# Four instructions in other places of the engines' lists: exponentials, a layer norm's shift, bias pieces and LSTM weight sums

## The chip, the cores and the metric

The kernel runs on one core of a Trainium2 chip. The metric is the time of one execution on the device in microseconds, as the median of several runs. All data are fp32. A core has five engines with a queue of instructions each: TensorE (matmul; in the profile PE, and PEld for its loads of weights), VectorE (DVE), ScalarE (ACT), GpSimd (POOL) and SyncE (SP, which issues the DMA transfers here).

## What is computed

A stack of four graph layers on x of 128 graphs with 64 nodes and 256 features, with one 64x64 adjacency. Each layer is "x = x + layer(relu(layernorm(x)))".

```python
# --- layer 0 ---   two graph convolutions, then LSTMs over windows of 1, 2, 3, 4 nodes
h = relu(einsum('ts,bsh->bth', adj, h @ Wg0 + bg0))
h = relu(einsum('ts,bsh->bth', adj, h @ Wg1 + bg1))
for p in range(1, 5):            # the last hidden state replaces the window's last node
    h = h.at[:, idx, :].set(lstm_last(Wih[p-1], Whh[p-1], ..., windows(h, p)))
# --- layer 1 ---   normalized adjacency, two linear layers with batch norm
# --- layer 2 ---   three weights, for diagonal, upper and lower part of adj, and a bias
out = adj_0 @ (x @ W[0]) + adj_1 @ (x @ W[1]) + adj_2 @ (x @ W[2]) + bias
# --- layer 3 ---   masked attention over the 64 nodes of a graph
scores = q @ k.T * scale + adj_mask          # causal
y = softmax(scores) @ v @ Wo
```

## The kernel before

The 8192 rows are cut into 16 tiles of 512 rows (number s). There are three long stages: graph rounds (layer 0 up to the LSTM, one tile each round), the LSTM steps with layer 1 after them, and a last stage for layers 2 and 3, which takes the tiles in 8 pairs.

The order of each engine's instructions is planned by hand. Every piece of work is entered in a list with a planned time, `at(t, function, ...)`; the list is sorted by this time and the functions are called in that order. A planned time is therefore no moment, only a place: it decides which instruction stands before which in the queue of its engine. What an instruction waits for is set by its data.

```python
def at(t, fn, *args):
    events.append((t0 + t, len(events), fn, args))
...
for _, _, fn, args in sorted(events, key=lambda e: e[:2]):
    fn(*args)
```

**A graph round** (`t0 = 10 * s`). Layer norm: statistics on VectorE, the root on GpSimd (power of -0.5), the shift on VectorE, relu on ScalarE:

```python
def root(qs):
    rn = v["rn"][:, 0, qs]
    nc.vector.tensor_scalar_add(rn, v["mv"][:, qs, 1], EPS)
    nc.gpsimd.tensor_tensor(rn, rn, mhalf[:, : qs.stop - qs.start], ALU.pow)      # L318
def shift(qs):
    nc.vector.scalar_tensor_tensor(v["rn"][:, 1, qs], v["mv"][:, qs, 0], -1.0,     # L321
                                   v["rn"][:, 0, qs], op0=ALU.mult, op1=ALU.mult)
def relu(q):
    nc.scalar.activation(v["h"][:, q, :], v["xt"][:, q, :], AF.Relu, ...)          # L325
```

Then the first convolution (`aggregate0`, L333, with a ScalarE copy out of the bank, L337; `weigh`, L343; `weighed`, the add of a bias out of the bank, L349 on VectorE; `relu1`, L354 on ScalarE), the second aggregation with the same two lines, and the second weight in a form of Strassen's with seven products, one round later:

```python
for k in range(2):
    at(late + 6.56 + 1.72 * k, weigh, k)
    at(late + 8.3 + 1.75 * k, weighed, k)
    at(late + 8.9 + 1.75 * k, relu1, k)
late += ROUND          # 10
...                    # aggregate0 of "g1" with its copies
for k in range(4):
    at(late + (7.2, 7.9, 8.0, 8.05)[k], sums, k)     # GpSimd, L364
late += ROUND
for t, name, j in ((0, "c", 2), (0.43, "a", 1), (1.75, "b", 5), (2.18, "a", 6),
                   (3.5, "b", 3), (3.93, "a", 7), (6.1, "a", 4)):
    at(late + t, product, name, j)                   # TensorE, L372
at(late + 0.5, begun, 0, 0, "c")                     # VectorE, L379
at(late + 0.9, add, 0, 0, "a")                       # VectorE, L386
at(late + 2.3, begun, 1, 1, "b")
...
if s == 9:
    for k in range(4):
        at(0.6 + 1.6 * k, lambda k=k: weight_sum(wih0[0], k))   # GpSimd, L279
```

Product a6 adds to bank a, which `add(0, 0, "a")` must have read before. b5 and the products before it don't wait for that add.

**A pair of the last stage** (`t0 = 52.5 * i`, tiles 2i and 2i+1). In the order of one tile: norm of x2 to h2 (root L967, shift L970, relu L974), the bias added to x2 by GpSimd (`biased`, L987), the graphs of layer 2 (`graphs3`, matmuls L999, copies L1004 on ScalarE and VectorE), the weights (L1011), the sum (`weighed`, L1017), norm to h3, transposes (L1024), then seven products for q k (`qproduct`, L1051) with ScalarE copies (`qcopy`, L1055) and VectorE adds (`qadd`, L1058) and four products for v (`hv`, L1075, copied at L1079), scores (L1085), mask (L1090), row maximum (L1095), exponentials, their transposes, and the last product:

```python
def exps(q):
    nc.scalar.activation(v["sc"][:, q, :], v["sc"][:, q, :], AF.Exp,              # L1098
                         bias=v["mx"][:, 0, q : q + 1], accum_out=v["mx"][:, 1, q : q + 1])
...                       # turn_e: transposes L1106, turned_e: copy L1110; attend: L1116, attended: L1121
u = 0.43
for k, (name, j) in ((0, ("c", 2)), (1, ("a", 1)), (4, ("b", 5)), (5, ("a", 6)),
                     (8, ("b", 3)), (9, ("a", 7)), (13, ("a", 4))):
    at(t_QH + k * u, qproduct, name, j)
for q, k in enumerate((2, 6, 10, 14)):
    at(t_QH + k * u, hv, q)
at(t_QH + 2 * u, qcopy, 0, 0, "a")
at(t_QH + 3 * u, qadd, 0, 0, "c")
at(t_QH + 5.1 * u, qcopy, 1, 1, "b")
at(t_QH + 6.1 * u, qcopy, 0, 1, "a")
at(t_QH + 8 * u, hv_copy, 0)
at(t_QH + 10.1 * u, qadd, 1, 1, "a")
at(t_QH + 10.2 * u, qadd, 0, 1, "b")
at(t_QH + 14.1 * u, qcopy, 1, 0, "a")
at(t_QH + 16 * u, hv_copy, 1)
at(t_S, scores)
at(t_S + 2, masked)
at(t_soft, largest)
for q in range(Q):
    at(t_soft + 0.7 + 0.6 * q, exps, q)
... # turn_e at t_E, attend and attended from t_O
```

Products b3 and a7 need that `qcopy` has read bank b and bank a. The even tile's scores and exponentials (t_S = 40.0, t_soft = 42.7) lie among the odd tile's products (t_QH = 42.0).

Of the kernel before, what the change touches and what calls it, by code (L numbers as in the profile page):

```python
# [20 lines left out]
def kernel(ctx: ExitStack, tc: tile.TileContext, a: dict, out: bass.AP):  # L21
# [255 lines left out]
    def weight_sum(w, k):  # L277
        op = nc.gpsimd.tensor_sub if k else nc.gpsimd.tensor_add
        op(*(w[:, m] for m in ((S1, A21, A22), (S2, S1, A11), (S3, A11, A21), (S4, A12, S2))[k]))  # L279
# [10 lines left out]
    ROUND, HALF = 10.0, SUP // 2  # L290
    with tc.tile_pool(name="pa", bufs=2) as pa, tc.tile_pool(name="pax", bufs=3) as pax:
        events, wih0, made = [], [], []

        def graph_part(s):
            t0, v = ROUND * s, {}

            def at(t, fn, *args):
                events.append((t0 + t, len(events), fn, args))
# [118 lines left out]
                    at((-15.1, -14.5, -13.1, -12.5)[q], stats, q)  # L417
            for qs, t in halves:
                at(t, root, qs)
                at(t + 1.4, shift, qs)  # L420
                for q in range(qs.start, qs.stop):
                    at((2.7 - ROUND if s == 1 else t + 1.5) + 0.6 * (q - qs.start), relu, q)
            late, end = 0, s == NS - 1
            for c in range(KC):
                at(late + 0.86 + 1.75 * c, aggregate0, "g0", "h", c)
# [6 lines left out]
            for c in range(KC):  # L432
                t = (0.86, 2.6)[c] if end else 4.35 + 0.89 * c
# [38 lines left out]
                at(5.0, lambda: normalize(made[0]))  # L472
            if s == 9:
                for k in range(4):
                    at(0.6 + 1.6 * k, lambda k=k: weight_sum(wih0[0], k))

        for s in range(NS):
            graph_part(s)
# [60 lines left out]
    def at(t, fn, *args):  # L539
        events.append((t, len(events), fn, args))  # L540
# [169 lines left out]
    t = 0.0  # L710
    wt[0][0].append(wih0[0])
    for p in range(1, NL + 1):
# [8 lines left out]
        for k in range(0, len(pairs), 2):  # L721
            sts = [{"blk": blk, "N": blk[0][2] * GB, "p": p, "pool": pool}
                   for blk, pool in zip(pairs[k : k + 2], (lh0, lh1))]
            for j in range(p):
                for st in sts:
# [4 lines left out]
                    t = step(t, st, j, j == p - 1, l, wt[l], turn)  # L730
# [187 lines left out]
    NP = NS // 2  # L918
    with tc.tile_pool(name="pc", bufs=2, reuse_waits="tile") as pc, \
# [3 lines left out]
        def rest(s, at, only_pair, t_T, t_n, t_G, t_W, t_h, t_QH, t_S, t_soft, t_E, t_O, end):  # L923
# [6 lines left out]
            def q2s(k):  # L930
                return slice(2 * k, 2 * k + 2)
# [20 lines left out]
            def norm(src, tag, halves, t_rows, t_relu):  # L952

                def new():
                    v["st"] = pc.tile([P, Q, 6], F32, tag="ln_st", name="ln_st", bufs=4)
                    v["mv"] = pc.tile([P, Q, 2], F32, tag="ln_mv", name="ln_mv", bufs=4)
                    v["rn"] = pc.tile([P, 2, Q], F32, tag="ln_rn", name="ln_rn", bufs=4)
                    v[tag] = pc.tile([P, Q, D], F32, tag=tag, name=tag)

                def stats(q):  # L960
                    nc.vector.bn_stats(v["st"][:, q, :], v[src][:, q, :])
                    nc.vector.bn_aggr(v["mv"][:, q, :], v["st"][:, q, :])
# [11 lines that stand above are left out]
                    nc.scalar.activation(v[tag][:, q, :], v[src][:, q, :], AF.Relu,  # L974
                                         bias=v["rn"][:, 1, q : q + 1], scale=v["rn"][:, 0, q : q + 1])

                at(t_rows[0] - 0.01, new)
                for q in range(Q):
                    at(t_rows[q // 2] + 0.6 * (q % 2), stats, q)
                for k, qs in enumerate((q2s(0), q2s(1)) if halves else (slice(0, Q),)):  # L980
                    at(t_relu[k] - 1.5, root, qs)
                    at(t_relu[k] - 0.1, shift, qs)
                    for q in range(qs.start, qs.stop):
                        at(t_relu[k] + 0.6 * (q - qs.start), relu, q)
# [150 lines left out]
            if first_:  # L1135
                norm("x2", "h2", True, (t_T + 0.455, t_T + 1.8), (t_T + 3.2, t_T + 4.6))
                for q in range(Q):
                    at(t_T + 7 + 0.7 * q, biased, q)
            else:
                norm("x2", "h2", False, (t_n, t_n + 1.2), (t_n + (11.9 if s % 2 and s > 1 else 4.1),))  # L1140
                for q in range(Q):
                    at(t_n + (14.5 if s % 2 else 10.5) + 0.7 * q, biased, q)
            for k in range(4):
                at(t_G + 0.8 * k, graphs3, *((k % 2, k // 2) if first_ else (k // 2, k % 2)))
            for k in range(2):
# [33 lines left out]
            at(t_S + 2, masked)  # L1179
            at(t_soft, largest)  # L1180
            for q in range(Q):
                at(t_soft + 0.7 + 0.6 * q, exps, q)
            for k, qs in enumerate((q2s(0), q2s(1)) if end else (slice(0, Q),)):
                at(t_E + 0.2 * k, turn_e, qs)
                at(t_E + 0.2 * k + 0.1, turned_e, qs)
# [4 lines left out]
        for i in range(NP):  # L1190
            t0, first_, end = PERIOD * i, i == 0, i == NP - 1

            def at(t, fn, *args, t0=t0):
                events.append((t0 + t, len(events), fn, args))

            rest(2 * i, at, i, -8.6 if first_ else -40.2, -38.3, 0, (7.0, 12.6), 29.0, 32.6, 40.0, 42.7,
                 46.3 if end else 46.5, 50.4 if end else 48.85, False)
            if first_:
                at(-7.6, weight_product, 2, wo, wvo)
            rest(2 * i + 1, at, i, -3.0 if first_ else -27.6, 1.5 if first_ else -25.4, 12.3 if first_ else 3.5, (17.8, 26.5), 39.1,  # L1200
                 (42.0, 45.4, 48.7, 49.6, 52.1) if end else 42.0, 46.7 if end else 50.6,
                 49.5 if end else 59.5, 53.0 if end else 64.7, 53.8 if end else 75.6, end)
        for _, _, fn, args in sorted(events, key=lambda e: e[:2]):
            fn(*args)
# [38 lines left out]
```

## Time and profile before

The median of three runs is 1910.28 us (1909.95 to 1910.47). The profiled execution spans 1908.6 us.

| what | value |
|---|---|
| ScalarE copy of half a bank (L1055) | 0.37 us each |
| exponential of 128x128 (L1098) | 0.39 us, and 0.19 us to read its sum |
| GpSimd root of 128x4 (L967) | 1.0 us |
| bias piece on GpSimd (L987), 128x256 | 0.7 us |
| LSTM weight sum on GpSimd (L279), 128x512 | 1.3 us |
| graph rounds repeat every | 10.49 us |
| pairs of the last stage repeat every | 52.49 us |

How to read the views: the page's first part gives, for each engine, its busy time, the share of the span and the number of instructions. A list of waits says which engine and line waited for which other, with the total in us, how often, and the longest. A timeline gives start (us from the start of the span), length (us), engine, line, operation, what is written and read, the shape, and in brackets the idle time before the instruction with what ended it. Busy time over a stretch is given for all engines in one row. L numbers are lines of the kernel before.

### The profile page before, as it was taken

The numbers are of one execution on the slowest core, as the hardware profiler recorded it, in microseconds if no ns is written. First come the engines' busy times: TensorE is split into PE (matmuls) and PEld (weight loads), VectorE is DVE, ScalarE is ACT, GpSimd is POOL, SyncE is SP. The second block draws the span as 40 slices with busy tenths as digits, with TensorE's granted clock in tenths as the row PEclk, the third lists the DMA queues.
The fourth block names the chain that finished last, engine by engine and source line by source line (L and its number), as shares of the span: only waits on it lengthen the run. The fifth ranks groups of instructions, "written<-read, shape, count | busy, mean of one in ns | idle before, by whom it ended". The sixth has DMA issues, their size and how long they took to land.

```text
span 1908.6 us, 19724 instructions
## 1 busy us (share of the span) xinstructions
PE 1872.3 (98%) x7112; PEld 1174.0 (62%) x7112; DVE 1142.5 (60%) x2264; ACT 890.0 (47%) x1539; POOL 612.5 (32%) x491
## 2 busy tenths in 40 slices
PE   8999999999999999999999999999999999999999
PEld 7887444444445666665444444555444888888887
DVE  6765777634546445435633334588786767666664
ACT  5765667534435444434533333444574433443442
POOL 4341322443324432422522224533053411211120
PEclk9999999999999999999999999999999999999999
DMA  4110000100001000000000001233100011111101
GB/s 138 56 56 1 1 1 15 30 1 0 1 0 45 1 0 1 1 0 23 0 0 1 1 0 35 87 111 110 64 1 22 23 45 45 45 34 45 45 23 34
DMA packets 49539, 54.34 MB, mean 28 GB/s; under 512 B 3105, under 2 KB 44833, under 8 KB 49441
## 3 DMA queue, kind: packets, MB, share of 16 engines
q1 hardware_dynamic: 48976, 52.87, 8.8%
q8 instruction: 57, 0.93, 0.2%
q14 instruction: 42, 0.34, 0.1%
q10 hardware_dynamic: 464, 0.20, 0.0%
HBM read 36.28 MB, written 16.78 MB: 28 GB/s over the span
## 4 chain that ended last, share of the span: by engine, by line
PE 88%; DVE 6%; POOL 3%; ACT 3%; issue 1%; DMA 0%; ACTq 0%; DVEq 0%; POOLq 0%
PE ps L605 34%; PE ps L611 19%; PE ps L1011 8%; PE ps L521 6%; PE ps L841 5%; PE ps L999 2%; PE ps L1075 2%; PE ps L1051 2%; PE ps L333 2%; PE ps L372 2%; PE ps L219 1%; PE ps L1116 1%; POOL t L364 1%; DVE tq L1038 1%; PE ps L1085 1%; PE ps L229 1%
## 5 line engine op out<-in xcount | busy, mean ns | idle before, releaser
L627 DVE TENSOR_TENSOR gate<-gate,ps 128x512 f32<-128x512 f32 (+2 forms) x378 | 224.1, 620 | 446.1 <-PE ps L611 366.8
L605 PE MATMUL ps<-tx,wih 128*128 128x512 f32 (+2 forms) x1008 | 446.8, 542 | 2.8 <-ACT gate L630 1.2
L605 PE MATMUL ps<-hT,wih 128*128 128x512 f32 (+2 forms) x756 | 338.5, 541 | 0.0
L630 ACT COPY gate<-ps 128x512 f32<-128x512 f32 (+2 forms) x252 | 134.5, 534 | 378.5 <-PE ps L611 325.0
L605 PEld LDWEIGHTS ps<-tx,wih 128*128 128x128 f32 x1008 | 190.5, 190 | 193.0 <-issue 130.8
L623 ACT ACTIVATE gate<-gate,lbias 128x512 f32<-128x512 f32 (+2 forms) x252 | 216.7, 860 | 157.5 <-DVE gate L627 157.5
L611 PE MATMUL ps<-h,whh 128*128 128x512 f32 (+2 forms) x576 | 256.6, 527 | 0.0
L605 PEld LDWEIGHTS ps<-hT,wih 128*128 128x128 f32 x756 | 143.6, 190 | 141.6 <-issue 79.6
L611 PE MATMUL ps<-th,whh 128*128 128x512 f32 (+2 forms) x432 | 192.5, 527 | 0.0
L1011 PE MATMUL ps<-wl,ag 128*128 128x256 f32 x768 | 172.1, 380 | 0.0
L611 PEld LDWEIGHTS ps<-h,whh 128*128 128x128 f32 x576 | 109.4, 190 | 100.2 <-issue 76.5
L650 POOL TENSOR_TENSOR gate<-gate 128x1024 f32<-128x1024 f32 (+2 forms) x36 | 71.8, 2016 | 304.7 <-ACT gate L623 304.7
L1011 PEld LDWEIGHTS ps<-wl,ag 128*128 128x128 f32 x768 | 143.4, 190 | 20.2 <-ACT ag L1004 1.8
L650 POOL TENSOR_TENSOR cell<-gate 128x1024 f32<-128x1024 f32 (+2 forms) x36 | 79.4, 2227 | 175.2 <-ACT gate L623 175.2
L967 POOL TENSOR_TENSOR ln_rn<-ln_rn,mhalf 128x4 f32<-128x4 f32 (+1 forms) x33 | 32.8, 994 | 311.0 <-DVE ln_rn L966 310.5
L611 PEld LDWEIGHTS ps<-th,whh 128*128 128x128 f32 x432 | 82.1, 190 | 75.2 <-issue 57.4
L974 ACT ACTIVATE h<-x,ln_rn 128x256 f32<-128x256 f32 x128 | 68.2, 593 | 104.2 <-DVE ln_rn L970 104.2
L521 PE MATMUL ps<-ag,w 128*128 128x512 f32 x256 | 112.3, 592 | 0.0
L650 POOL TENSOR_TENSOR cell<-gate,cell 128x1024 f32<-128x1024 f32 (+2 forms) x32 | 65.1, 2052 | 109.4 <-ACT gate L623 109.4
L630 DVE COPY gate<-ps 128x512 f32<-128x512 f32 (+2 forms) x126 | 78.6, 624 | 20.8 <-PE ps L611 20.8
L655 ACT ACTIVATE gate<-cell 128x1024 f32<-128x1024 f32 (+2 forms) x72 | 68.1, 952 | 29.5 <-POOL cell L650 29.5
L623 ACT ACTIVATE gate<-ps,lbias 128x512 f32<-128x512 f32 (+2 forms) x126 | 79.6, 632 | 3.9 <-PE ps L611 1.0
(213 smaller groups left out, 2820.4 us busy)
## 6 DMA issues: line engine op xcount, KB each, us to landing
xt<-in_x_dram SPq DMA_DIRECT2D x30, 512.0 KB, 4.4
x1d<-xt SPq DMA_DIRECT2D x16, 512.0 KB, 3.0
x<-x1d SPq DMA_DIRECT2D x16, 512.0 KB, 5.1
out_dram<-x SPq DMA_DIRECT2D x15, 512.0 KB, 3.2
wih<-in_WihT_dram SPq DMA_DIRECT2D x16, 256.0 KB, 4.8
whh<-in_WhhT_dram SPq DMA_DIRECT2D x12, 256.0 KB, 5.2
xt<-in_x_dram SPq DMA_DIRECT2D x8, 128.0 KB, 3.8
wl<-in_W_dram SPq DMA_DIRECT2D x3, 256.0 KB, 3.1
```

The lines of the kernel that those rows point to most:

```text
L333: nc.tensor.matmul(p_[:, ts(q, P)], v[h][:, q, ts(c, P)], adjT_bd, start=True, stop=True)
L521: nc.tensor.matmul(p_, con["w1"][:, c, ts(o, P)], ag[:, c, :], start=(c == 0), stop=(c == KC - 1))
L605: nc.tensor.matmul(wide(p_[:, :N]), wih[0][:, OF[k], gi, :], x_, start=first_, stop=(j == 0), skip_group_check=True)
L611: nc.tensor.matmul(p_[:, :N], whh[0][:, OF[k], gi, :], h_, start=False, stop=True, skip_group_check=True)
L623: nc.scalar.activation(to, r[bank_][:, :N] if bank_ else to, fn, bias=lbias[:, l, m : m + 1])
L627: nc.vector.tensor_add(slot(n, hc), slot(n, hc), r[bank_][:, :N])
L630: op(slot(n, hc), r[bank_][:, :N])
L650: fn(*((t["G"] if isinstance(t, dict) and "G" in t else st["c"])[:, n, :, : st["N"]] for t in tiles))
L655: nc.scalar.activation(o_, c, AF.Tanh)
L841: nc.tensor.matmul(banks[name], w2[:, OF[j], k, :], x_, start=(new and k == 0), stop=(k == 1), skip_group_check=True)
L974: nc.scalar.activation(v[tag][:, q, :], v[src][:, q, :], AF.Relu, bias=v["rn"][:, 1, q : q + 1], scale=v["rn"][:, 0, q : q + 1])
L1011: nc.tensor.matmul(v["W"][:, q, :], v["ag"][:, c, m, ts(2 * k + q, P)], wl2[m][:, c, :], start=(n == 0), stop=(n == 3 * KC - 1))
```

## The change

It moves four things in the lists and leaves the computation and the number of instructions as they were.

- In the graph rounds the shift of the layer norm and its relus are entered 1.6 later, from the third tile on, so that VectorE's and ScalarE's queues have other work before them while GpSimd forms the root.
- The LSTM weight sums on GpSimd get other slots in the tenth round.
- In the last stage the exponentials of the even tile are entered 1.4 later (not in the last pair), behind ScalarE's copies of the odd tile's banks. The transposes of the exponentials and the product after them move back by about 2, and the odd tile's scores move ahead of that product.
- The bias pieces of the odd tiles are entered 3.5 later.

```diff
             for qs, t in halves:
                 at(t, root, qs)
-                at(t + 1.4, shift, qs)
+                at(t + (1.4 if s < 2 else 3.0), shift, qs)
                 for q in range(qs.start, qs.stop):
-                    at((2.7 - ROUND if s == 1 else t + 1.5) + 0.6 * (q - qs.start), relu, q)
+                    at((2.7 - ROUND if s == 1 else t + (1.5 if s == 0 else 3.1)) + 0.6 * (q - qs.start), relu, q)
...
             if s == 9:
                 for k in range(4):
-                    at(0.6 + 1.6 * k, lambda k=k: weight_sum(wih0[0], k))
+                    at(1.4 + 1.3 * k, lambda k=k: weight_sum(wih0[0], k))
...
                 for q in range(Q):
-                    at(t_n + (14.5 if s % 2 else 10.5) + 0.7 * q, biased, q)
+                    at(t_n + (18 if s % 2 else 10.5) + 0.7 * q, biased, q)
...
             for q in range(Q):
-                at(t_soft + 0.7 + 0.6 * q, exps, q)
+                at(t_soft + (0.7 if s % 2 or only_pair == NP - 1 else 2.1) + 0.6 * q, exps, q)
...
     # even tile: ..., t_h, t_QH, t_S, t_soft, t_E, t_O
             rest(2 * i, at, i, ..., 29.0, 32.6, 40.0, 42.7,
-                 46.3 if end else 46.5, 50.4 if end else 48.85, False)
+                 46.3 if end else 48.46, 50.4 if end else 50.85, False)
     # odd tile: t_QH, t_S
-                 (42.0, 45.4, 48.7, 49.6, 52.1) if end else 42.0, 46.7 if end else 50.6,
+                 (42.0, 45.4, 48.7, 49.6, 52.1) if end else 42.0, 46.7 if end else 48.9,
```

## The prediction

> **What bounds the kernel now.** I read the page's first part and its waits first, then asked for busy time by stage, then for the chain of waits and the timeline of one repeat in each stage that the change touches.
>
> ```profile
> PE 1872.3 (98%) x7112; PEld 1174.0 (62%) x7112; DVE 1142.5 (60%) x2264; ACT 890.0 (47%) x1539; POOL 612.5 (32%) x491
> ```
>
> ```profile
> 20.00:176.00 156.00, 151.78 (x915) 135.72 (x915) 101.19 (x265) 104.07 (x171) 60.60 (x78) 1.00 0.18 52
> 176.00:1476.00 1300.00, 1292.57 (x3670) 663.75 (x3669) 737.39 (x1200) 613.25 (x933) 459.21 (x283) 1.00 0.06 20
> 1476.00:1909.00 433.00, 416.03 (x2469) 363.84 (x2467) 291.63 (x752) 162.35 (x417) 84.30 (x106) 1.00 0.12 38
> ```
>
> The first line says that TensorE is the bound; nothing can be won that is not an idle moment of PE. The three stages (columns: stretch, length, then busy time of PE, PEld, DVE, ACT, POOL) say where idle moments are: 4 us in the graph rounds (20 to 176), 7 us in the LSTM with the first products after it (176 to 1476), which no edited line touches except one weight sum ahead of it, and 17 us in the last stage. Each matmul row is drawn about 0.17 us too long (a 0.43 us pair of rows shows as 0.60), so a gap is really larger than the idle time says; I count gaps from start to start instead.
>
> What ends those gaps, from the list of waits, PE alone (us in total, times, longest):
>
> ```profile
> PE ps L1051 <- ACT qk L1055: 7.9, 7, 1.1
> PE ps L372 <- DVE h L386: 4.1, 12, 1.3
> ```
>
> The change goes at exactly these two. The first is once in each pair of the last stage but the last pair (seven times), the second once in nearly every graph round.
>
> **What the Trainium skill says.** "PSUM — Partial Sum Buffer", section "Engine vs sequencer instructions": the queues of ScalarE, VectorE and GpSimdE are strict FIFO. So an instruction that waits holds back all that follow it, though they are ready, and moving it later in the list can free them; but a move that passes no other instruction of its own engine does nothing. The trace agrees: the 0.16 us shift at 67.10 below holds a ready add behind it. "SBUF — State Buffer", "Who interferes with whom": a VectorE instruction with two SBUF inputs contends with a GpSimd instruction that reads SBUF, and the loser blocks for the whole instruction. The trace agrees: the same shift takes 0.16 us alone and 1.22 us beside a weight sum. The same two sections give me all I use; for every duration I take the trace.
>
> **The graph rounds: shift and relu later (s ≥ 2).** The timeline of one round, us from the start, us long, engine, line:
>
> ```profile
> 66.05 1.01 POOL L318 TENSOR_TENSOR ln_rn<-ln_rn,mhalf 128x4 f32<-128x4 f32 x1
> 66.36 1.03 PE L372 MATMUL ps<-g,wg 128*128 128x256 f32 x4
> 67.10 0.16 DVE L321 SCALAR_TENSOR_TENSOR ln_rn<-ln_mv,ln_rn 128x4 f32<-128x4 f32 x1 [1.07 <-POOL ln_rn L318]
> 67.18 0.68 DVE L349 TENSOR_TENSOR h<-ps,rsb 128x512 f32<-128x512 f32 x1
> 68.11 0.60 PE L372 MATMUL ps<-t,wg 128*128 128x256 f32 x2
> 68.35 0.42 DVE L386 TENSOR_TENSOR h<-h,ps 128x256 f32<-128x256 f32 x1
> 68.92 0.67 PE L372 MATMUL ps<-t,wg 128*128 128x256 f32 x2 [0.21 <-DVE h L386]
> ```
>
> GpSimd's root (L318) stands behind its four sums and ends at 67.06. DVE's shift (L321) waits for it, and behind it in DVE's queue stand `weighed(1)` (L349), `begun` (L379) and the `add` (L386) that product a6 needs. PE could have begun a6 at 68.11 + 0.43 = 68.54; it began at 68.92, and paid 0.08 more for restarting (the next row begins 0.51 and not 0.43 later): 0.46 us lost. By the plan's times modulo the round of 10, the shift moves from 9.5 to 1.1: behind `weighed(1)` (0.05), `begun` (0.5) and `add` (0.9). `weighed(1)`'s matmuls end at 66.36, 66.56 with the 0.20 that such a hand-over takes here; then 0.6 + 0.4 + 0.1 + 0.42 in DVE's queue gives 68.1, and 0.15 to PE 68.25, before 68.54. The wait is gone with 0.3 us to spare. The relus go to 1.2 to 3.0, about a microsecond later in fact; the first matmul that reads them is at 77.72, six microseconds after they end, and ScalarE has four short copies beside them.
>
> The 12 waits: at 27.00 it is 27.00 − 26.06 = 0.94 us; at 37.44, 0.32; nine of 0.46 = 4.1; and the one beside the LSTM weight sums:
>
> ```profile
> 98.52 3.84 POOL L279 TENSOR_TENSOR wih<-wih 128x512 f32<-128x512 f32 x3
> 98.59 1.22 DVE L321 SCALAR_TENSOR_TENSOR ln_rn<-ln_mv,ln_rn 128x4 f32<-128x4 f32 x1 [1.08 <-POOL ln_rn L318]
> ```
>
> Here the shift is blocked by the weight sum (1.22 us), and a6 begins at 101.47 instead of 100.02: 1.5 us with the restart. Moved behind the add it may still be blocked, but then only the next `begun`, which has 0.4 to 0.6 us of slack; I leave 0.2 us of the 1.5 there. One round more gains: in round 10, relus of s = 2 stand before `relu1(1)` (18.15), which PE waits for at 18.82; with the relus behind it, PE is next held by the g0 copy, which ends about 0.8 us earlier by ScalarE's list. Sum: 0.94 + 0.32 + 4.1 + 1.3 + 0.8 = **7.5 us**.
>
> **The weight sums at s = 9.** From 0.6 + 1.6k to 1.4 + 1.3k. On GpSimd they stand after the root at 8.1 of the round before and before the sums at 7.2, in the old and in the new slots. A planned time is only a place in the list, so GpSimd's list does not change, and the instructions are on no other engine: **0 us**.
>
> **The bias pieces.** For odd s from t_n + 14.5 to t_n + 18. From the second pair on this is 45.1 to 47.2 of a pair instead of 41.6 to 43.7, and GpSimd has nothing between 37.5 and the next pair's 16.8: same list, **0 us**. Only s = 1 differs: its pieces 1 to 3 fall behind the root of h3 (19.9) of the first pair. That root began when DVE's input came, not when GpSimd was free, so it gains nothing; `weighed` of s = 1 then waits for piece 1, at about 1508.15 instead of 1508.03. I put 0.1 us against it.
>
> **The exponentials behind the bank copies.** One pair:
>
> ```profile
> 1632.15 0.69 DVE L1095 TENSOR_REDUCE mx<-sc 128x4 f32<-128x512 f32 x1
> 1632.87 0.40 ACT L1098 ACTIVATE sc<-sc,mx 128x128 f32<-128x128 f32 x1 [2.07 <-DVE mx L1095]
> 1633.66 0.35 ACT L1055 COPY qk<-ps 128x256 f32<-128x256 f32 x1
> 1634.06 0.70 PE L1051 MATMUL ps<-h3T,aqk 128*128 128x256 f32 x2 [1.13 <-ACT qk L1055]
> 1634.31 0.35 ACT L1055 COPY qk<-ps 128x256 f32<-128x256 f32 x1
> 1634.71 0.70 PE L1051 MATMUL ps<-tq,aqk 128*128 128x256 f32 x2
> ```
>
> ScalarE sits 2.07 us before the first exponential of the even tile because the row maximum is late, and the copies of banks b and a of the odd tile, ready since about 1631.7 and 1632.1, stand behind it. PE finishes `hv(1)` at 1631.90 + 0.86 = 1632.76 and waits for the first copy to 1634.06 (1.30 us). b3 and a7 then take 1.35 us by the chain's own starts (a7 waits for the second copy, and both restart cold), where the same four rows without a wait take 0.86: 0.49 more. So 1.30 + 0.49 = 1.8 us stand in each pair.
>
> After: copies at 1631.7 and 1632.1, end 1632.45; b3 at 1632.76, a7 at 1633.19, hv at 1633.62, a4 at 1634.48. a4 needs DVE's add of bank a: 1633.62 + 0.20 + 0.41 + 0.15 = 1634.4, just in time. The exponentials still begin at 1632.87 (two take 0.79), the hv copy lies between (0.5), the last ends at about 1635.05. The transposes of the exponentials now stand behind the last hv, at 1635.78: 0.7 us to spare. The odd scores come next (48.9, ahead of attend at 50.85): their copy is done at about 1635.5, they run from 1636.2 to 1638.0, attend to 1639.7, and graphs of the next pair begin there, where they began at 1641.45. What this may give back: DVE's first graph copy (52.5) stands before `attended(1)` (52.61), so the bank of the second attend is free only at about 2.4 us after the graph stage begins, and the eighth graph bank needs it at 2.2: 0.2 us. Net 1.6 us. In the first pair the exponential's table load (1.28 us, at 1526.1, hidden in the wait now) comes behind the copies, and pushes the exponentials past the transposes by some 0.3 us: net 1.3. The last pair keeps its old times. Sum: 6 × 1.6 + 1.3 = **10.9 us**.
>
> **Total**: 7.5 + 10.9 − 0.1 = 18.3 us; 1910.3 − 18.3 = 1892.0.
>
> **Rivals.**
> (1) *The wait is only exchanged.* In the last stage the row maximum comes no earlier; if PE's next need, a4's add or the transposes, waits instead, little comes out. For it: the a4 margin is 0.1 us. Against it: the transposes stand 0.7 us after the last exponential. With half the gain lost there, 1897.
> (2) *Buffers pass it on.* The graph stage starts 1.7 us earlier and meets DVE's `attended` and its own copies; PE could stall on banks for more than the 0.2 us I allow. For it: copies run at PE's pace there (ScalarE waits 0.17 us for each). 0.5 us a pair would make 1894.
> (3) *The moved relus collide.* In the graph rounds g0's second copy now stands behind three relus of 0.5 us; if the weights that read it waited, the round would keep its 10.49 us, and the time would be about 1899. Against it: the copy would end near 71.0 and is read at 73.4.
> (4) *Bias and weight sums do matter*, through the shared port rather than the list. I see no way while GpSimd's list is unchanged.
>
> **Range and chances.** Losing one of the two large terms in part gives the upper end, 1898; all waits gone with no give-back (1.8 × 7 + 8) gives 1889 to 1890, and a little for gaps I did not count 1888. All of PE's idle time in both stages is about 30 us, so 2% (38 us) is out of reach: faster by over 2% 0.01, within 2% 0.985, slower by over 2% 0.005.
>
> **What would show it.** Graph rounds 10.03 us apart instead of 10.49 and no a6 waiting on L386; shift rows without a wait. In the last stage pairs some 50.9 us apart instead of 52.49, no L1051 waiting for L1055, the exponentials still ending the row maximum's wait. GpSimd's rows as before but for the first pair. The LSTM stage unchanged, only earlier by 7 to 8 us. Wrong would be: pairs at 52 us with PE waiting for L1098 or L1121, or rounds that stay at 10.4 us with a wait on L337.

## The result, and the profile after

The changed kernel takes 1891.24 us (median of 4 runs, 1890.40 to 1891.49) where the kernel before takes 1910.38: a ratio of 0.9899, 95% interval 0.9882 to 0.9917, about 19 us. The profiled span went from 1908.6 to 1889.8 us.

First part of the page of the changed kernel, and its busy time over the three stages (stretch, length, busy time of PE, PEld, DVE, ACT, POOL):

```profile
PE 1865.3 (99%) x7112; PEld 1174.5 (62%) x7112; DVE 1141.4 (60%) x2264; ACT 891.6 (47%) x1539; POOL 611.9 (32%) x491
...
20.00:168.50 148.50, 148.07 (x910) 136.45 (x911) 99.95 (x264) 104.42 (x172) 60.61 (x78) 1.00 0.18 54
168.50:1468.00 1299.50, 1292.07 (x3667) 663.33 (x3666) 737.35 (x1200) 613.16 (x933) 458.36 (x283) 1.00 0.06 20
1468.00:1890.00 422.00, 413.03 (x2471) 364.20 (x2469) 291.78 (x752) 163.71 (x417) 84.62 (x106) 1.00 0.12 39
```

Every engine does the same number of instructions in nearly the same busy time. The stretches are cut at about the same places of the program in both kernels. By these cuts the graph rounds lost 7.5 us and show almost no idle PE now (148.07 of 148.50), the LSTM stretch is as long as it was, and the last stage lost 11 us.

One graph round of the changed kernel, from its timeline; the rows answer to those shown of before:

```profile
53.26 1.00 POOL L318 TENSOR_TENSOR ln_rn<-ln_rn,mhalf 128x4 f32<-128x4 f32 x1
53.57 1.03 PE L372 MATMUL ps<-g,wg 128*128 128x256 f32 x4
53.77 0.69 DVE L349 TENSOR_TENSOR h<-ps,rsb 128x512 f32<-128x512 f32 x1 [0.53 <-PE ps L343]
54.95 0.42 DVE L386 TENSOR_TENSOR h<-h,ps 128x256 f32<-128x256 f32 x1
55.29 0.16 DVE L321 SCALAR_TENSOR_TENSOR ln_rn<-ln_mv,ln_rn 128x4 f32<-128x4 f32 x1
55.32 1.03 PE L372 MATMUL ps<-t,wg 128*128 128x256 f32 x4
```

`weighed(1)` (L349) now waits only for its own matmuls and begins 0.20 us after the four rows at 53.57 do (before: 0.82). The add (L386) ends at 55.37, the shift stands behind it and waits for nothing. Products b5 and a6 run as one block of four rows at 55.32, with no gap between them. From one such block to the next it is 10.05 us: the rows of L343 that open the weights lie at 50.28, 60.33, 70.37, 80.42 in the chain of waits.

One pair of the last stage of the changed kernel, from its timeline:

```profile
1620.92 0.81 ACT L1055 COPY qk<-ps 128x256 f32<-128x256 f32 x2 [0.87 <-PE ps L1051]
1621.40 0.69 DVE L1095 TENSOR_REDUCE mx<-sc 128x4 f32<-128x512 f32 x1
1622.02 0.59 PE L1051 MATMUL ps<-h3T,aqk 128*128 128x256 f32 x2
1622.12 0.40 ACT L1098 ACTIVATE sc<-sc,mx 128x128 f32<-128x128 f32 x1 [0.39 <-DVE mx L1095]
1622.45 0.59 PE L1051 MATMUL ps<-tq,aqk 128*128 128x256 f32 x2
...
1625.04 0.60 PE L1106 MATMUL ps<-ident,sc 128*128 128x128 f32 x4
```

The row maximum comes no earlier in the pair than before. But both bank copies are done before ScalarE begins to wait for it, so b3 and a7 follow each other by 0.43 us. ScalarE's own wait for the maximum shrank from 2.07 to 0.39 us because it works during it; the transposes (L1106) stand late enough that the last exponential is through. Busy time over one whole pair, first of the kernel before, then of the changed one:

```profile
1588.96:1641.45 52.49, 51.36 (x309) 45.45 (x309) 36.57 (x94) 20.00 (x52) 10.10 (x12) 1.00 0.13 41
```

```profile
1578.20:1629.08 50.88, 50.88 (x309) 45.46 (x308) 36.59 (x95) 20.24 (x52) 10.08 (x12) 1.00 0.13 42
```

The same 309 matmul rows, in 50.88 us instead of 52.49, and no idle PE drawn.

### The profile page after: what moved, and what is told of

Same layout as the page of the kernel before. It is cut to its first block, busy times and chain, and to the rows that moved or that the text cites. A ratio compares the mean times of both kernels' runs of the same rounds, so it can differ in the third digit from the quotient of the medians.

```text
span 1889.8 us, 19741 instructions
## 1 busy us (share of the span) xinstructions
PE 1865.3 (99%) x7112; PEld 1174.5 (62%) x7112; DVE 1141.4 (60%) x2264; ACT 891.6 (47%) x1539; POOL 611.9 (32%) x491
## 4 chain that ended last, share of the span: by engine, by line
PE 94%; DVE 3%; ACT 1%; POOL 1%; DMA 0%; issue 0%; ACTq 0%; DVEq 0%; POOLq 0%
PE ps L605 34%; PE ps L611 19%; PE ps L1011 8%; PE ps L521 6%; PE ps L841 5%; PE ps L1075 3%; PE ps L343 3%; PE ps L333 3%; PE ps L372 2%; PE ps L1051 2%; PE ps L999 2%; PE ps L1085 2%; PE ps L219 2%; PE ps L1116 1%; PE ps L1024 1%; PE ps L229 1%
## 5 line engine op out<-in xcount | busy, mean ns | idle before, releaser
L974 ACT ACTIVATE h<-x,ln_rn 128x256 f32<-128x256 f32 x128 | 68.3, 594 | 103.1 <-DVE ln_rn L970 103.1
L521 PEld LDWEIGHTS ps<-ag,w 128*128 128x128 f32 x256 | 47.6, 190 | 54.5 <-issue 52.1
```

What stands on the lines that cost most here:

```text
L521: nc.tensor.matmul(p_, con["w1"][:, c, ts(o, P)], ag[:, c, :], start=(c == 0), stop=(c == KC - 1))
```

## The experiments

The theory: two waits of TensorE were queue waits. An instruction that waits for slow work (GpSimd's root, the row maximum) stood in its engine's queue ahead of ready ones that TensorE needed. Moving shift and relus, and moving the exponentials with what follows them, accounts for all; the bias pieces and the weight sums change nothing. The rivals: the parts only work together; ScalarE's relus rather than VectorE's shift were the obstacle; TensorE's new order has a worth of its own; the bias pieces matter by blocking VectorE (rival 4 of the prediction).

| run | edit | median us | kernel before, measured beside it | ratio (95%) |
|---|---|---|---|---|
| e1 | shift and relus | 1902.72 | 1911.01 | 0.9956 (0.9944 to 0.9969) |
| e2 | exponentials and reorder | 1899.85 | 1911.01 | 0.9941 (0.9929 to 0.9954) |
| e3 | bias pieces, weight sums | 1911.08 | 1911.01 | 1.0001 (0.9993 to 1.0009) |
| e4 | relus alone | 1911.35 | 1911.01 | 1.0003 (0.9994 to 1.0011) |
| e5 | exponentials alone (one too late) | 1900.22 | 1910.79 | 0.9947 (0.9934 to 0.9959) |
| e6 | reorder alone | 1910.99 | 1910.79 | 1.0001 (0.9993 to 1.0009) |
| e7 | e1 and e2 together | 1891.49 | 1910.79 | 0.9900 (0.9887 to 0.9914) |
| e8 | the changed kernel, one more copy later | 1889.94 | 1910.79 | 0.9893 (0.9877 to 0.9908) |
| e9 | before, root twice | 1928.48 | 1910.64 | 1.0090 (1.0074 to 1.0107) |
| e10 | the changed kernel, root twice | 1892.23 | 1910.64 | 0.9901 (0.9886 to 0.9916) |
| e11 | exponentials alone, all in time | 1902.51 | 1910.96 | 0.9955 (0.9942 to 0.9969) |

**e1, shift and relus alone.**

```diff
-                at(t + 1.4, shift, qs)
+                at(t + (1.4 if s < 2 else 3.0), shift, qs)
-                    at((2.7 - ROUND if s == 1 else t + 1.5) + ..., relu, q)
+                    at((2.7 - ROUND if s == 1 else t + (1.5 if s == 0 else 3.1)) + ..., relu, q)
```

> The kernel before with the later shift and relus of the graph rounds alone. Queue theory (the shift that waits for GpSimd's root held three VectorE instructions and through them product a6): rounds 10.05 us apart instead of 10.49, no a6 waiting on L386, about 1902.7 us (7.6 less). Rival (the four moves only work together, or a later stage eats the gain): 1907 or more. The last stage keeps its pairs of 52.49 us.

It is 8.3 us less than the kernel before that was measured beside it. Rounds are 10.05 us apart, the list of waits has no L372 any more and still has the seven of L1051, and pairs stay at 52.5 us. The gain of this part stands alone.

**e2, exponentials and reorder alone.**

```diff
-                at(t_soft + 0.7 + 0.6 * q, exps, q)
+                at(t_soft + (0.7 if s % 2 or only_pair == NP - 1 else 2.1) + 0.6 * q, exps, q)
-   even tile: t_E 46.5, t_O 48.85     odd tile: t_S 50.6
+   even tile: t_E 48.46, t_O 50.85    odd tile: t_S 48.9
```

> The kernel before with the later exponentials and the new places of their transposes, the odd scores and the attend product alone. Queue theory: pairs 50.88 us apart, about 1.6 us less in each of seven pairs, 1899.2 us (11.1 less), graph rounds still 10.49 us. Rival (the bias pieces of GpSimd were part of it through the shared port): pairs above 51.2 us, 1902 or more.

It is 11.2 us less, with pairs 50.88 us apart and eleven of the twelve waits of L372 still there. The bias pieces were not part of it. The two parts add: 8.3 + 11.2 = 19.5 us, and both together (e7) gave 19.3.

**e3, bias pieces and weight sums alone**, and **e7, all but these.**

```diff
-                    at(0.6 + 1.6 * k, lambda k=k: weight_sum(wih0[0], k))
+                    at(1.4 + 1.3 * k, lambda k=k: weight_sum(wih0[0], k))
-                    at(t_n + (14.5 if s % 2 else 10.5) + 0.7 * q, biased, q)
+                    at(t_n + (18 if s % 2 else 10.5) + 0.7 * q, biased, q)
```

> The kernel before with the later bias pieces and the LSTM weight sums in other slots alone. Queue theory: GpSimd's list is the same but for three pieces in the first pair, so 1910.3 us within 0.4. Rival (the pieces run at other moments and block VectorE less): 1 to 3 us less, 1907.5 to 1909.5.

> The kernel before with shift and relus, exponentials and the reorder, but with the bias pieces and the weight sums in their old places. Queue theory: as the changed kernel, 1891.3 us within 0.4. Rival (bias and weight sums matter once the waits are gone): 1893 or more.

There is no difference either way: 1911.08 against 1911.01, and without these edits 1891.49 (the changed kernel took 1891.24). The order of GpSimd's rows in the traces says why. It differs from that of the kernel before in one place, the first pair, where three pieces of the second tile stand behind one more root; the weight sums stand where they stood. In the timeline of e3 the weight sums still begin as the root ends, 0.99 us after its start, as they did before (97.53 and 98.52):

```profile
98.31 1.02 POOL L318 TENSOR_TENSOR ln_rn<-ln_rn,mhalf 128x4 f32<-128x4 f32 x1
99.30 5.08 POOL L279 TENSOR_TENSOR wih<-wih 128x512 f32<-128x512 f32 x4
```

**e4, relus later, shift in its old place.** The edit is the second pair of lines of e1.

> The kernel before with only the relus of the graph rounds later, the shift in its old place. Queue theory (VectorE's queue held by the shift is the cause): nothing changes in the rounds, 10.49 us apart, 1910.3 us within 0.5. Rival (ScalarE's relus ahead of the bank copies were the cause): about 1903 to 1905 us.

Nothing came out, and L372 waits for L386 twelve times, 4.6 us in all. ScalarE's relus were not the obstacle. They read the shift's result, so they come later when it does; the shift without a new place for the relus was not run.

**e9 and e10, the root twice**, in the kernel before and in the changed one.

```diff
+                v["rx"] = pa.tile([P, Q], F32, tag="ln_rx", name="ln_rx", bufs=3)
...
                 nc.vector.tensor_scalar_add(rn, v["mv"][:, qs, 1], EPS)
+                if s > 1:
+                    nc.gpsimd.tensor_tensor(v["rx"][:, qs], rn, mhalf[:, : qs.stop - qs.start], ALU.pow)
                 nc.gpsimd.tensor_tensor(rn, rn, mhalf[:, : qs.stop - qs.start], ALU.pow)
```

> The kernel before with GpSimd's root of the graph rounds done twice (from the third tile on; the first result goes to a tile that nobody reads), so that it ends 1.0 us later. Queue theory: the shift and what stands behind it come 1.0 us later, and a6 with them, in 12 rounds: rounds 11.5 us apart, about 1922 us. Rival (GpSimd's root is not on the path): 1910 to 1912.

> The changed kernel with the root twice in the same way. Queue theory: the shift now stands behind the add, about 1.0 us after the root ends, so the whole extra microsecond is hidden: 1891.2 us within 1, rounds 10.05 us apart. Rival: the late root costs here too, 1897 or more.

This tests the mechanism itself: if the shift no longer stands ahead of the add, a slower root must be free. It nearly is (1892.23, 1.0 us more than the changed kernel's median), while the kernel before pays 17.8 us. The chain of waits of the kernel before shows how the root sets the length of a round (main pieces of one round):

```profile
66.10 0.98 POOL ln_rn L318
67.10 0.16 DVE ln_rn L321
68.35 0.43 DVE h L386
68.92 0.67 PE ps L372 x2
72.33 0.59 ACT g L337
74.49 2.10 POOL t L364 x3
76.58 0.98 POOL ln_rn L318
```

It is a closed loop through four engines: root, shift and add, product a6, the copy out of the bank, GpSimd's sums, and the next root. The loop takes 76.58 − 66.10 = 10.48 us, the length of a round, so a longer root lengthens every round by as much. In the changed kernel the chain runs through matmuls alone in nearly all of these rounds. Timeline of e9 (three edited lines shift the numbers by 3: L321 is the second root, L324 the shift, L389 the add, L375 the products):

```profile
74.92 1.01 POOL L321 TENSOR_TENSOR ln_rn<-ln_rn,mhalf 128x4 f32<-128x4 f32 x1
75.97 0.16 DVE L324 SCALAR_TENSOR_TENSOR ln_rn<-ln_mv,ln_rn 128x4 f32<-128x4 f32 x1 [2.85 <-POOL ln_rn L321]
77.22 0.42 DVE L389 TENSOR_TENSOR h<-h,ps 128x256 f32<-128x256 f32 x1
77.79 0.67 PE L375 MATMUL ps<-t,wg 128*128 128x256 f32 x2 [1.66 <-DVE h L389]
```

and of e10:

```profile
74.85 1.01 POOL L321 TENSOR_TENSOR ln_rn<-ln_rn,mhalf 128x4 f32<-128x4 f32 x1
75.45 0.42 DVE L389 TENSOR_TENSOR h<-h,ps 128x256 f32<-128x256 f32 x1
75.90 0.17 DVE L324 SCALAR_TENSOR_TENSOR ln_rn<-ln_mv,ln_rn 128x4 f32<-128x4 f32 x1
```

In e9 VectorE sits idle for 2.85 us before the shift, the add begins 1.25 us after the shift, and TensorE waits 1.66 us for it. In e10 the add runs at 75.45 while the second root is still at work; that root ends at 75.86, just as the shift comes up.

The 12 us that I expected for e9 were too few, though its rounds are as long as expected. From its chain, the roots of five rounds and one run of matmuls:

```profile
51.38 1.02 POOL ln_rn L321
62.97 1.02 POOL ln_rn L321
74.92 1.02 POOL ln_rn L321
86.51 1.02 POOL ln_rn L321
98.10 1.02 POOL ln_rn L321
...
116.89 1.72 PE ps L336 x8
```

Most rounds are 11.59 us long, 1.10 more than before, which is the second root (the first begins at 73.83, the second at 74.92: 1.09). The total is larger for three reasons. Thirteen rounds grew and not twelve: about 14.2 us. In two of them, the first and the one beside the weight sums, TensorE waited 1.86 and 2.37 us for the add, and the clock that it was granted, which the profile gives as a share of full speed, then read 0.50 (30.5 to 32.5 us, and 115.8 to 118.3), so that eight rows of L336 took 1.72 us where they take 0.89 otherwise; that cost another 1.66 us in each. In the other eleven rounds the waits were 1.09 to 1.66 us and the clock read 1.00; why it fell in those two was not tested. The third reason is the round shown above, which took 11.95 us: the second of GpSimd's sums began 0.50 us after the copy that it waits for, and 0.14 us after it in the next round. Its cause stays open. Together this is the 17.9 us by which the thirteen rounds of the profiled execution grew.

In e10 the rounds are 10.05 us apart as in the changed kernel, but for the first (10.15) and the one beside the weight sums (10.41 instead of 10.27). So the rounds account for 0.24 us of the 1.0; the profiled executions differ by 0.5 us, and the other 0.3 lies ahead of the first round, where all versions scatter.

**e6, the reorder of TensorE alone; e5 and e11, the exponentials alone.** e6 has the new t_E, t_O and t_S of e2 without its first edit; e5 has only that first edit. In e5 the fourth exponential's time (46.6) is just past its transposes' (46.5). So e5 leaves out the last exponential of the even tile in what it transposes: the last quarter is the masked scores, and TensorE doesn't wait for the fourth exponential. e11 has all four in time, by a spacing of 0.55; the order in every engine's list is that of e5.

> The kernel before with the transposes of the exponentials, the odd scores and the attend product in their new places, the exponentials in the old. My theory: products b3 and a7 wait for the bank copies as before, and nothing else waited, so 1910.3 us within 0.5. Rival (the new order of TensorE is itself worth something): 1 to 4 us less.

> The kernel before with the exponentials later, but their transposes, the odd scores and the attend product in their old places. My theory: the wait for the bank copies goes, but the transposes now stand right behind the third hv product and wait some 0.6 us for the last exponential: about 1.1 us less a pair, nothing in the first (table load), so some 7 us less, 1903.5 us. Rival 1 (the reorder is not needed): 1899. Rival 2 (without it the wait is only exchanged): 1909 or more.

> As e5_exps_alone, with all four exponentials ahead of their transposes in the list (spaced 0.55 instead of 0.6), so that the transposes wait for the fourth too; the order of every engine's instructions is that of e5. My theory: the transposes, right behind the third hv product, now wait some 0.6 us for the last exponential, in six pairs (in the first the table load makes it more): some 3.5 us above e5, 1903.7 us. Rival (the last exponential is not on TensorE's path even there, the reorder is not needed): 1900.2 us as e5.

The reorder alone is worth nothing: PE's wait for the copies is as before (7.9 us, 7 times). The exponentials alone bring 8.5 us (e11), with pairs of 51.16 us; with the reorder 11.2 (e2) and 50.88. So the reorder is needed for the remaining 2.7 us, and e5, which took away the data dependence and not the place, has pairs of 50.89. Which of its parts does it, the later transposes or the earlier odd scores, was not run separately; the wait that it removes is that of the transposes. I had expected a stall of 0.6 us a pair in e11; it is 0.28. The timeline of e11 shows why:

```profile
1632.89 0.89 PE L1106 MATMUL ps<-ident,sc 128*128 128x128 f32 x4
1632.91 0.39 ACT L1098 ACTIVATE sc<-sc,mx 128x128 f32<-128x128 f32 x1
...
1633.44 0.14 PEld L1106 LDWEIGHTS ps<-ident,sc 128*128 128x128 f32 x1 [0.24 <-ACT sc L1098]
```

The transposes go one by one: three of four run while the last exponential does, and only the fourth waits, 0.24 us. Most of the rest of the 2.7 us is the first pair: from the first L999 row of its graphs to the next pair's it takes 52.06 us in e11 against 50.88 in e2. There the load of the exponential's table comes behind the copies, and the list of waits of e11 has L1106 waiting 0.5 us for L1098, once.

**e8, one more of the same kind.** In both kernels the transposes of h3 (L1024) waited about 0.2 us a pair for the last two relus (L974), ahead of which ScalarE copied a bank of hv (L1079, 0.56 us) that nobody needed yet.

```diff
-                at(t_QH + 8 * u, hv_copy, 0)
+                at(t_QH + (8 if s % 2 else 11.5) * u, hv_copy, 0)
```

So that the later copy still reads its own bank, the two banks of hv have names of their own in e8 (`v["H", k]` instead of `v["H"]`).

> The changed kernel with the even tile's first copy of hv (0.56 us on ScalarE) behind the last two relus of the odd tile's h3, which the transposes L1024 wait for by 0.22 us in each pair. The same reading as for the exponentials: pairs 50.66 us apart instead of 50.88, 1.3 to 1.5 us less, 1889.8 us. Rival (the statistics before the relus set that wait, or the copy is missed elsewhere): 1891.2 us or more.

From the timeline of the changed kernel, then of e8:

```profile
1614.56 0.56 ACT L1079 COPY hw<-ps 128x512 f32<-128x512 f32 x1
1615.03 1.09 ACT L974 ACTIVATE h<-x,ln_rn 128x256 f32<-128x256 f32 x2
...
1615.69 1.25 PE L1024 MATMUL ps<-ident,h 128*128 128x128 f32 x8
```

```profile
1613.07 2.07 ACT L974 ACTIVATE h<-x,ln_rn 128x256 f32<-128x256 f32 x4 [1.18 <-DVE ln_rn L970]
1615.05 0.56 ACT L1079 COPY hw<-ps 128x512 f32<-128x512 f32 x1
1615.20 1.04 PE L1024 MATMUL ps<-ident,h 128*128 128x128 f32 x8
```

Four relus in one run, the eight transposes without a break, pairs of 50.67 us instead of 50.88: 1889.94 us against the 1891.49 of e7, measured beside it. It is the fastest version here.

## Why the prediction was right

**The total** (1892.0, measured 1891.24) and both terms hold: 7.5 us for the graph rounds, 10.9 for the last stage. By the trace, the first matmul of the last stage's graphs moved from 1483.97 to 1476.34 us, 7.6 us, and the rest of the span shortened by 11.2. The mechanism is the predicted one in both stages. That the terms agree so closely is in part luck, since errors cancel in each.

**Shift and relu.** Predicted rounds of 10.03 us; they are 10.05. The add was to end 1.74 us after the block of c2 and a1 begins; it ends 1.80 us after it (55.37 − 53.57). The round beside the weight sums lost the whole wait: from a6 at 89.91 to a6 at 101.47 it had taken 11.56 us. In the chain of the changed kernel it takes 10.27 from 93.92 to 104.19, 0.22 of which is an extra matmul that fell into the next round before. The shift there is a row of 0.25 us at 95.48, not 1.22. It came up near the end of a weight sum, and the 0.2 us that I had left for a blocked `begun` were not lost. The 0.8 us for round 10 were too many: the second block of weights (L343) still waits 0.39 us for the copy L337, and the first block of c2 and a1 begins at 23.42 instead of 23.88, 0.46 us earlier. Even this is about the scatter of the start: that block begins between 23.56 and 24.62 in the seven traces with the shift in its old place and one root, and between 23.42 and 23.66 in the four with the new place. The rounds after it made up for the shortfall. They gave 7.2 us (the same block of the last round is at 164.32 instead of 171.96, 7.64 us earlier, less 0.46) where the prediction's other terms sum to 6.7. Its waits at 27.00 and 37.44 leave out the restart (the rounds lost 1.01 and 0.38, not 0.94 and 0.32), the one beside the weight sums gave 1.5 and not 1.3, and the round after that one lost a further 0.24 us that the list of waits doesn't show.

**Bias pieces and weight sums.** A loss of 0.1 and 0 us was predicted; e3 measured a loss of 0.07 with an interval of about ±1.5. For these moves e3 and e7 show that a planned time which passes no other instruction of its engine does nothing. The 0.1 us of the first pair can't be told from zero.

**The exponentials.** 1.6 us a pair predicted, 52.49 − 50.88 = 1.61 measured; but two errors cancel in it. The first is the term for b3 and a7, "0.49 more". I read it off the chain, where a row starts at the drawn end of the row before, which is late. By the timeline's starts b3 to hv took 1635.25 − 1634.06 = 1.19 us instead of 0.86, so 0.33, and the wait was 1.63 us and not 1.8. The second is the 0.2 us that banks should have cost. VectorE did take its first graph copy before `attended(1)`, as foreseen, and that ended 2.34 us after the graphs began, but the 64 rows of L999 took 5.40 us as before. So that bank was not missed, and rival 2 got nothing. The margin of 0.1 us at a4 held (no wait of L1051 is left in the list but one of 0.4 us in the first pair, which was there before). In the first pair I gave back 0.3 us for the table load; the pair went from 52.50 to 50.97 us, 1.53 less, so nearly nothing was given back.

**The rivals.** The wait was not exchanged: PE's list has nothing new but 0.6 us of L343 in the start-up. The moved relus did not collide: the second g0 copy ends at 58.1 in the round above, two microseconds before the weights at 60.33 begin.

## What to carry to other kernels

With hand-ordered queues, look for an instruction whose bracket shows a wait and ask what stands behind it in the same queue: if one of those is ready and on the bound engine's path, it belongs ahead, even if the waiting one is short. After such a move, check the next consumer: moving the exponentials alone brought 8.5 us, and giving TensorE something else to do until the last of them was through brought 2.7 more. Before a move is tried, count which instructions of its own engine it passes: if there are none, expect nothing, as with the weight sums and most of the bias pieces here.

## What I had not expected

Four transposes behind four exponentials stall by 0.24 us and not by the 0.6 us that I had expected between the end of hv and the last exponential, because each waits for its own quarter only (e11). And an extra microsecond on GpSimd ahead of a waiting shift came back whole in each of thirteen rounds, and with 1.66 us on top in the two where TensorE's clock fell after the wait (e9), while it cost about 1 us in the whole kernel once the shift stood behind the add (e10).
